# Four graph layers on one core: attention's bf16 adjacency masks are cast in layer 1 and kept in DRAM, and the first head's second half sums by comparisons

## The chip, the cores and the metric

The kernel runs on one core of one Trainium2 chip. The core has TensorE (PE, matrix products into PSUM), VectorE (DVE), ScalarE (ACT), GpSimd (POOL) and SyncE (SP), which work side by side and wait for each other by semaphores. SyncE, ScalarE and GpSimd also issue DMAs, each into a queue of its own; one set of 16 DMA engines serves all of them. The metric is the device time of one execution in microseconds, as the median of several runs. One execution was also taken with the hardware profiler; durations here come from it.

## The reference

x is 2708 x 512, `adj` is a symmetric 0/1 matrix of 2708 x 2708 with about 2.4% ones and a diagonal of ones. Four layers follow each other, each as `h = relu(layernorm(x)); x = x + layer(h, adj)`:

- layer 0: `relu((adj.T @ h) @ W * deg**-0.5)`;
- layer 1: the mean over the first 64 neighbours of each row, and two dense products with leaky ReLU;
- layer 2: graph attention with 8 heads of 64, the layer that this change is about;
- layer 3: the mean over all neighbours, and two dense products.

Layer 2, per head:

```python
Wh = h @ W                                   # 2708 x 64
e  = leaky_relu(f1[:, None] + f2[None, :], 0.2)   # f1 = Wh @ a1, f2 = Wh @ a2
p  = softmax(where(adj > 0, e, -9e15), axis=-1)
out = elu(p @ Wh)
```

## The kernel before

**Chunks.** Rows are cut into NC = 22 chunks of R = 128 (the last has 20). The adjacency is kept in SBUF as uint8, `vT[g][:, k, :]`: for each chunk m of neighbours, 2708 columns of nodes.

**Layer 1's aggregation.** `aggregate` walks seven spans of at most four chunks of columns; in each, for every m, `weight1(m, cs)` lets VectorE make a 128 x 512 weight `kt` (the first 64 neighbours), and TensorE multiplies by it into PSUM (`acc`). `after1` finishes the chunks of the span before, and `save2` stores them as x2 from ScalarE's queue. The tile `hT` (two buffers of the pool `common`) is used by the dense products before and after, not here.

**Attention.** The weight of neighbour m for node n is exp(leaky_relu(f1 + f2)) = exp(f2) * exp(0.2 f1) * max(exp(0.8 f1), exp(-0.8 f2)). `make(s)` lets VectorE compute `max(row, ec) * vT` in one instruction (tile `t2`, four buffers, line 1089); `scale(s)` lets ScalarE scale Wh by exp(f2) (`whs`, line 1073); `multiply(s)` multiplies the two on TensorE in four column groups of 32 (line 1348): `av` is the weighted sum, and `sums`, from one6, a column of ones, is the softmax's denominator.

A step s is one chunk m of one unit u. The units are head 0 in two parts (columns 0 to 1408, then 1300 more), heads 1 to 6 whole, and head 7 in two parts: 10 units of 22 steps. Weights are made three steps ahead. The last chunk's 20 rows of heads 1 to 6 are done together (`load_tails`, `exp_tails`, `make_tails`: `tails_row` is 120 x 2708).

**Sums by comparisons.** For chunks in `BY_SIDE` (17 of them, m % 5 != 2) of units 2 to 8 the f32 `sums` matmul is replaced: ScalarE makes a bf16 comparison tile b from the weight (`compare`, Sigmoid with a huge scale, line 1107), and `multiply_sides`, a step later, multiplies it by `parts`, exponentials split into three bf16 values, in bf16. What neighbours without comparison add is the same for every unit up to a factor per head, so `count_neighbors(i)` sums it once for all heads: the adjacency of chunk BY_SIDE[i] as bf16 (`mask(i, j)` for four quarters j of the columns, `fourths` = 0, 704, 1408, 2058, 2708) times `parts2`, into two PSUM banks `adj_sums`. Masks are cast from uint8 by ScalarE into one of five `x` tiles (line 1412); the last quarter of the later chunks is cast by VectorE into one of two `mask` tiles (line 1409). A count is 8 bf16 matmuls (line 1424).

**Order.** Steps are written out one after another; everything else hangs behind a step by `behind(step, fn, ...)`. `behind(1 + 39 * i // 16 + j // 2, mask, i, j)` and two steps behind the first `count_neighbors(i)` spread the 17 counts over the 44 steps of units 0 and 1. A scheduler then fixes the order of each engine's instructions from dependencies, this order as priority, and its own estimate of times; each engine works in that order. `issue_after` keeps an instruction behind another one.

Of the kernel before, what the change touches and what calls it, by code (L numbers as in the profile page):

```python
# [8 lines left out]
F32 = mybir.dt.float32  # L9
F32R = mybir.dt.float32r  # L10
BF16 = mybir.dt.bfloat16
# [9 lines left out]
P = 128  # L21

R = 128
# [21 lines left out]
def fast_layers(  # L45
# [36 lines left out]
    nc = tc.nc  # L82
    N, D = x_in.shape
    H, _, O = w2.shape
    NC = -(-N // R)
    NF = D // P
# [5 lines left out]
    def rows(c):  # L92
        return min(R, N - c * R)
# [17 lines left out]
    XBUFS = 5  # L111
    EARLY = NC // 2
# [8 lines left out]
    dram = ctx.enter_context(tc.tile_pool(name="dram", bufs=1, space=DRAM))  # L121

    common = ctx.enter_context(tc.tile_pool(name="common", bufs=2))
# [281 lines left out]
    vT = []  # L405
# [5 lines left out]
    where = {c: (g, k) for g, cs in enumerate(groups) for k, c in enumerate(cs)}  # L411

    def pattern(m, cs, n=R):

        g, k = where[m]
        v = vT[g][:n, k, cs[0] * R : (cs[-1] + 1) * R]
        return v.rearrange("p (c r) -> p c r", r=R)

    def by_chunk(t, cs):
        return t[:, : len(cs) * R].rearrange("p (c r) -> p c r", r=R)  # L420
# [56 lines left out]
    with ExitStack() as ring_ctx:  # L477
# [31 lines left out]
        with tc.tile_pool(name="l0", bufs=2) as wk, ExitStack() as ctx_l0:  # L509
            units = [(g, m) for g in range(len(groups)) for m in range(NC)]  # L510
# [364 lines left out]
        def fold(j):  # L875
# [9 lines left out]
                ALU.add,  # L885
            )

        def weight1(m, cs):
            kt = wk.tile([R, WG], F32R, name="kt", bufs=5)
            nc.vector.scalar_tensor_tensor(  # L890
                by_chunk(kt, cs),
                lastr[:, cs[0] * R : (cs[-1] + 1) * R].rearrange("p (c r) -> p c r", r=R),
                index[:R, m : m + 1],
                pattern(m, cs),
                op0=ALU.is_ge,
                op1=ALU.mult,
            )
            return kt
# [44 lines left out]

    BY_SIDE = [m for m in range(NC - 1) if m % 5 != 2]


    STEEP = 2.0**62
    ABOVE = 1.0 + 2.0**-21  # L950
    S = 32

    cut = EARLY * R // 8 * 8
    units = [(h, 0, N) for h in range(H)]
    units[-1:] = [(H - 1, 0, cut), (H - 1, cut, N)]
    units[:1] = [(0, 0, cut), (0, cut, N)]
# [3 lines left out]
    def in_tails(u, m):  # L960
# [2 lines left out]
    steps = [  # L963
        (u, m)
        for u in range(len(units))
        for m in ((NC - 1, *range(NC - 1)) if 1 < u < len(units) - 1 else range(NC))
    ]

    def by_side(u, m):
        return 1 < u < len(units) - 1 and m in BY_SIDE  # L970

    whd = dram.tile([N, D], F32, name="whd")
    avT = dram.tile([D, N], F32, name="avT")
# [15 lines left out]

    parts2 = at.tile([R, len(BY_SIDE), 2, H, 3], BF16, name="parts2")  # L990
    nc.gpsimd.memset(parts2, 0.0)
# [3 lines left out]
    row, weight, wh, whs, acc, sides, made, scaled = {}, {}, {}, {}, {}, {}, [], {}  # L995
# [52 lines left out]
    def load_wh(s):  # L1048
        u = steps[s][0]
        h = units[u][0]  # L1050
        t = at.tile([R, GROUP, O], F32, name="wh", bufs=3)
        ms = [m for v, m in steps[s : s + GROUP] if v == u and not in_tails(u, m)]
        full = [m for m in ms if m < NC - 1]
        k = len(full)
        for j, m in enumerate(sorted(ms)):
            wh[u, m] = t[:, j]
        if k:
            src = whd[full[0] * R : (full[0] + k) * R, h * O : (h + 1) * O]
            nc.sync.dma_start(t[:, :k], src.rearrange("(k p) o -> p k o", p=R))
        if k < len(ms):  # L1060
            src = whd[(NC - 1) * R :, h * O : (h + 1) * O]
            nc.sync.dma_start(t[:last_rows, k], src)

    def scale(s):

        u, m = steps[s]
        h, q = units[u][0], rows(m)
        if in_tails(u, m):
            whs[s] = tails_w[:LINES, middle.index(h)]
            return  # L1070
        t = at.tile([R, O + S], F32, name="whs", bufs=4)
        by = ef[:q, m, h : h + 1]
        ins = nc.scalar.activation(t[:q, :O], wh.pop((u, m))[:q], AF.Copy, scale=by)  # L1073
        if not by_side(u, m):
            ins = nc.scalar.activation(t[:q, O:], one6[:q], AF.Copy, scale=by)
        scaled[s] = ins.ins
        whs[s] = t[:q]

    def make(s):
        u, m = steps[s]  # L1080
        h, lo, hi = units[u]
        q = rows(m)
        g, k = where[m]
        if in_tails(u, m):
            weight[s] = tails_row[:LINES]
            made.append(made[-1])
            return
        t = at.tile([R, N], F32, name="t2", bufs=TILES)
        ins = nc.vector.scalar_tensor_tensor(  # L1089
            t[:q, : hi - lo],  # L1090
            row[h][:q, lo:hi],
            ec[:q, m, h : h + 1],
            vT[g][:q, k, lo:hi],
            op0=ALU.max,
            op1=ALU.mult,
        )
        weight[s] = t[:q]
        made.append(ins.ins)
# [91 lines left out]
    def split(first, end):  # L1190

        cs = slice(first, end)
        nc.scalar.mul(eb[:, cs], ec[:, cs], -STEEP * ABOVE)
        rest = common.tile([P, D], F32, name="rest", tag="t", bufs=3)
        rest = rest[:R, : (end - first) * H].rearrange("p (m h) -> p m h", h=H)
        for i in range(2):
            e = ef[:, cs]
            if i:
                nc.vector.tensor_tensor(rest, ec[:, cs], e, ALU.mult)
                e = rest  # L1200
            for k in range(3):
                part = parts_of[:, cs, :, 3 * i + k]
                nc.scalar.copy(part, e)
                if k < 2:
                    nc.vector.tensor_tensor(rest, e, part, ALU.subtract)
                    e = rest
        for i, heads in enumerate((slice(1, H), slice(1, H - 1))):
            kinds = sorted({m % 5 for m in BY_SIDE})
            for r in kinds:
                ms = [m for m in BY_SIDE if m % 5 == r and first <= m < end]  # L1210
                src = parts_of[:, ms[0] : ms[-1] + 1 : 5, heads, 3:6]
                at_i = [BY_SIDE.index(m) for m in ms]
                assert at_i == list(range(at_i[0], at_i[-1] + 1, len(kinds)))
                nc.scalar.copy(
                    parts2[:, at_i[0] : at_i[-1] + 1 : len(kinds), i, heads], src
                )
# [24 lines left out]
    def save_last2(c):  # L1241
# [7 lines left out]
    tails = tails_ctx.enter_context(  # L1249
        tc.tile_pool(name="tails", bufs=1, side="right", reuse_waits="tile")  # L1250
    )
# [140 lines left out]
                    t[j * step : j * step + height, : b - a],  # L1392
                )

    fourths = [0, cut // 2, cut, (cut + N) // 2, N]
    counted, masks = [], {}

    def pieces_of(j):
# [2 lines left out]
    def mask(i, j):  # L1401
        m = BY_SIDE[i]
        q = rows(m)
        g, k = where[m]
        own = slice(fourths[j], fourths[j + 1])
        n = own.stop - own.start
        if j == 3 and m >= EARLY:
            t = masks[i, j] = tails.tile([P, fourths[1]], BF16, name="mask", bufs=2)
            nc.vector.tensor_copy(t[:q, :n], vT[g][:q, k, own])
            return  # L1410
        t = masks[i, j] = common.tile([P, D], F32, name="x", bufs=XBUFS).bitcast(BF16)
        nc.scalar.copy(t[:q, :n], vT[g][:q, k, own])

    def count_neighbors(i):
        m = BY_SIDE[i]
# [37 lines left out]
    def behind(s, fn, *args):  # L1453
        plan.setdefault(s, []).append((fn, args))
# [5 lines left out]
    behind(10, load_row1, *units[1])  # L1460
    behind(9, split, EARLY, NC)
    behind(12, load_tails)
    behind(30, exp_tails)
    behind(36, make_tails)
    behind(30, load_l3_weights)
    behind(30, spread_nodes)
# [40 lines left out]
    for s in range(len(steps)):  # L1507
        if s == (len(units) - 3) * NC + 1:
            tails_ctx.close()
            first3 = ctx.enter_context(  # L1510
                tc.tile_pool(name="first3", bufs=1, side="right", reuse_waits="tile")
            )
            rings3 = [first3]
            b3 = first3.tile([P, D], F32, name="b3")
            nc.sync.dma_start(
                b3, bass.AP(tensor=bias3.tensor, offset=bias3.offset, ap=[[0, P], [1, D]])
            )
            e3_ctx = ctx.enter_context(ExitStack())
            e3 = e3_ctx.enter_context(
                tc.tile_pool(name="e3", bufs=2, side="right", reuse_waits="tile")  # L1520
            )
        if s + 6 < len(steps) and (s + 6) % NC % GROUP == 0:
            load_wh(s + 6)
        if s + 3 < len(steps):
            scale(s + 3)
            make(s + 3)
        if s + 1 < len(steps):
            compare(s + 1)
        multiply(s)
        multiply_sides(s - 1)  # L1530
        for fn, args in plan.pop(s, ()):
            if fn in (load_l3_weights, spread_nodes, split):
                with tc.issue_after(made[s]):
                    fn(*args)
            elif fn is mask:
                with tc.issue_after(scaled[s + 2]), tc.issue_after(made[s]):
                    fn(*args)
            else:
                fn(*args)
# [715 lines left out]
```

## Time and profile before

| | us |
|---|---|
| median of 3 runs | 1738.98 (1737.05 to 1739.90) |
| profiled execution, its own time | 1739.97 |
| profiled execution, span from first to last instruction | 1738.2 |
| first matmul of attention's unit 0, unit 1, unit 2 | 811.0, 860.0, 900.6 |
| TensorE busy | 1718.7 (99%) |
| VectorE busy | 1310.7 (75%) |
| ScalarE busy | 846.7 (49%) |
| GpSimd busy | 239.9 (14%) |
| DMA moved | 177.38 MB, mean 102 GB/s |

Times of instructions are counted from the span's start. Busy time is an average over stages, and the ends of the pipelined matmuls are modelled in the profile: TensorE at 99% does not say that TensorE is the limit everywhere. In rows of instructions in order of time, the bracket holds the engine's idle time before the instruction and what ended it. Records can overlap by some tens of nanoseconds where one instruction begins before the last has drained.

### The profile page before, as it was taken

What the parts mean: (1) busy time and instruction counts of PE and PEld (TensorE: products, weight loads), DVE (VectorE), ACT (ScalarE), POOL (GpSimd) and SP (SyncE); (2) the same over time, 40 slices, a digit from 0 to 9 for tenths busy, and PEclk for the clock granted to TensorE, in tenths of its full rate; (3) what the DMA queues carried; (4) which work ended last, traced back from release to release, by engine and by line L of the source; (5) the groups of instructions that cost most, each with busy time, mean ns of one, the idle gap of its engine ahead of it and who ended that gap; (6) DMA issues with size and microseconds to landing.
All of it is one profiled execution on the core that took longest, in us unless ns stands there. A gap on an engine that the chain in (4) does not pass through costs nothing.

```text
span 1738.2 us, 29482 instructions
## 1 busy us (share of the span) xinstructions
PE 1718.7 (99%) x11304; PEld 1074.6 (62%) x11304; DVE 1310.7 (75%) x1893; ACT 846.7 (49%) x1556; POOL 239.9 (14%) x246
## 2 busy tenths in 40 slices
PE   8999999999999999999999999999999999999998
PEld 5567777744458888644555676434434455588886
DVE  7759889865556756877899999999999777633334
ACT  5446767622210000266878888888885666400000
POOL 1003323311111111363000000000001222100000
PEclk9999999999999999999999999999999999999999
DMA  8436666444551111343420221122022444313221
GB/s 292 140 120 197 205 205 190 140 116 123 123 143 49 49 49 49 117 135 120 108 63 15 61 64 33 40 65 66 14 68 72 142 140 132 103 41 105 74 73 42
DMA packets 167228, 177.38 MB, mean 102 GB/s; under 512 B 84127, under 2 KB 106591, under 8 KB 166060
## 3 DMA queue, kind: packets, MB, share of 16 engines
q1 hardware_dynamic: 144428, 131.99, 27.2%
q10 hardware_dynamic: 18808, 33.37, 5.1%
q0 software_dynamic: 3840, 10.03, 1.5%
q8 instruction: 91, 1.49, 0.4%
q14 instruction: 61, 0.50, 0.1%
HBM read 111.64 MB, written 55.36 MB: 96 GB/s over the span
## 4 chain that ended last, share of the span: by engine, by line
PE 89%; DVE 6%; issue 2%; ACT 1%; SPq 1%; DMA 0%; DVEq 0%; ACTq 0%
PE acc L426 37%; PE av L1348 17%; PE nb_ps L188 8%; DVE t L1089 5%; PE h_ps L188 4%; PE wh_ps L188 4%; PE self_ps L188 4%; PE line_ps L188 4%; PE sums L1348 4%; PE hT_ps L247 2%; PE fused_ps L372 2%; ACT b L1107 1%; PE av_ps L1283 1%; DMA ws<-in_L_gnn_W_self 0%; PE sums_ps L633 0%
## 5 line engine op out<-in xcount | busy, mean ns | idle before, releaser
L1089 DVE SCALAR_TENSOR_TENSOR t<-rb,ec,vT 128x2708 f32<-128x2708 f32 (+2 forms) x214 | 513.2, 2457 | 12.5 <-PE sums L1348 9.8
L1348 PE MATMUL av<-t,whs 128*32 128x451 f32 (+5 forms) x4432 | 444.6, 514 | 3.4 <-DVE t L1089 2.1
L426 PE MATMUL acc<-halves,kt 128*128 128x512 f32 x1848 | 423.6, 390 | 1.0 <-DVE kt L890 1.0
L426 PEld LDWEIGHTS acc<-halves,kt 128*128 128x128 f32 x1848 | 346.0, 188 | 75.4 <-DVE kt L890 2.6
L1107 ACT ACTIVATE b<-t,eb 128x2708 bf16<-128x2708 f32 (+1 forms) x119 | 285.0, 2395 | 32.8 <-DVE t L1089 32.1
L1348 PEld LDWEIGHTS av<-t,whs 128*32 128x32 f32 (+1 forms) x4432 | 191.0, 110 | 165.3 <-issue 112.6
L426 PE MATMUL acc<-halves,ar 128*128 128x512 f32 x924 | 243.6, 414 | 0.0
L426 PEld LDWEIGHTS acc<-halves,ar 128*128 128x128 f32 x924 | 172.6, 188 | 58.2 <-issue 20.8
L224 ACT ACTIVATE ln_rs<-ln_mv,eps 128x1 f32<-128x1 f32 x88 | 25.7, 295 | 306.7 <-DMA x<-x 195.1
L890 DVE SCALAR_TENSOR_TENSOR kt<-lastr,index,vT 128x512 fp32r<-128x512 int16 (+3 forms) x154 | 110.6, 733 | 63.3 <-PE acc L426 62.9
L1572 DVE CAST kt<-vT 128x512 fp32r<-128x512 uint8 (+3 forms) x154 | 56.4, 368 | 130.7 <-PE acc L426 130.7
L1300 POOL TENSOR_SCALAR z<-y 128x512 f32<-128x512 f32 x22 | 44.1, 2006 | 642.2 <-DVE y L1293 642.2
L559 DVE TENSOR_TENSOR_SCAN cum<-ai,deg 128x512 int16<-128x512 int32 (+2 forms) x110 | 128.3, 1170 | 0.0
L602 ACT ACTIVATE cum<-cum,limit 128x512 int16<-128x512 int16 (+3 forms) x132 | 88.0, 667 | 52.0 <-DVE deg L567 49.8
L1348 PE MATMUL sums<-t,whs 128*32 128x325 f32 (+4 forms) x952 | 103.5, 448 | 0.0
L1073 ACT ACTIVATE whs<-wh,ef 128x64 f32<-128x64 f32 x214 | 72.7, 342 | 55.3 <-PE sums L1348 19.4
L220 DVE BATCH_NORM_STATS2 ln_st<-x 128x6 f32<-128x512 f32 x88 | 60.5, 689 | 48.9 <-DMA x<-x 34.9
L1348 PE MATMUL sums<-b,parts 128*32 128x338 bf16 (+2 forms) x884 | 76.8, 308 | 0.0
L188 PE MATMUL h_ps<-w0s,hT 128*128 128x512 f32 x168 | 75.8, 594 | 0.1
L188 PE MATMUL wh_ps<-w2s,hT 128*128 128x512 f32 x168 | 75.8, 594 | 0.0
L188 PE MATMUL self_ps<-wfs,hT 128*128 128x512 f32 x168 | 75.7, 593 | 0.0
L553 ACT ACTIVATE ar<-ai 128x512 fp32r<-128x512 int32 (+2 forms) x132 | 75.0, 568 | 1.4 <-DMA ai<-in_adj 0.9
(216 smaller groups left out, 1947.5 us busy)
## 6 DMA issues: line engine op xcount, KB each, us to landing
x<-x SPq DMA_DIRECT2D x105, 256.0 KB
ai<-in_adj SPq DMA_DIRECT2D x84, 256.0 KB
x<-x ACTq DMA_DIRECT2D x84, 256.0 KB
x<-in_x SPq DMA_DIRECT2D x42, 256.0 KB
rb<-rT SPq DMA_DIRECT2D x7, 1354.0 KB
wh<-whd SPq DMA_DIRECT2D x63, 96.0 KB
packed<-two POOLq DMA_DIRECT2D x44, 128.0 KB, 3.2
whd<-wh SPq DMA_DIRECT2D x21, 256.0 KB
```

The lines of the kernel that those rows point to most:

```text
L188: nc.tensor.matmul(po[:n], lhsT[:, f, :n], w[:, f, :], start=(f == 0), stop=(f == NF - 1))
L220: nc.vector.bn_stats(st[:n], xc[:n])
L426: nc.tensor.matmul(acc[:R], weight[:, k * R : (k + 1) * R], parts[:, i, :], start=(m == 0 and i == 0), stop=(m == NC - 1),)
L553: nc.scalar.activation(ar[:, :gw], ai[:, :gw], AF.Square, accum_out=squares[:R, m, g : g + 1])
L559: nc.vector.tensor_tensor_scan(cum[:n, :gw], ai[:n, :gw], ai[:n, :gw], 0.0 if g == 0 else deg[:n, m : m + 1], op0=ALU.add, op1=ALU.max,)
L602: nc.scalar.activation(cum[:n, :gw], cum[:n, :gw], AF.Sign, bias=limit[:n], scale=-1.0, accum_out=signs[:n, m, g : g + 1],)
L890: nc.vector.scalar_tensor_tensor(by_chunk(kt, cs), lastr[:, cs[0] * R : (cs[-1] + 1) * R].rearrange("p (c r) -> p c r", r=R), index[:R, m ...
L1073: ins = nc.scalar.activation(t[:q, :O], wh.pop((u, m))[:q], AF.Copy, scale=by)
L1089: ins = nc.vector.scalar_tensor_tensor(t[:q, : hi - lo], row[h][:q, lo:hi], ec[:q, m, h : h + 1], vT[g][:q, k, lo:hi], op0=ALU.max, op1=AL ...
L1107: nc.scalar.activation(b[:q, : hi - lo], weight[s][:, : hi - lo], AF.Sigmoid, bias=eb[:q, m, h : h + 1], scale=STEEP,)
L1348: nc.tensor.matmul(p[j * S : (j + 1) * S, : b - a], lhsT, rhs[:, part * size + a : part * size + b], start=(s % NC == 0), stop=(s % NC == ...
L1572: nc.vector.tensor_copy(by_chunk(kt, cs), pattern(m, cs))
```

## The change

1. All 68 masks (17 chunks x 4 quarters) are cast by ScalarE during layer 1's aggregation, one for each call of `weight1` from the 23rd on, into an `hT` tile, and stored from ScalarE's queue into a DRAM tensor `maskd`.
2. In attention `mask(i, j)` only loads: from `maskd` on GpSimd's queue, quarters 0 to 2 into `x` tiles, the last into a `mask` tile. ScalarE's and VectorE's casts are gone there, and so is the `issue_after` that held masks behind the scaling and the weight of a step.
3. Unit 1 (head 0's second part) also sums by comparisons for the 17 chunks; its last, 20-row chunk comes first, as in the later units, and `parts2` is filled for head 0 as well.
4. `exp_tails` hangs behind step 20 and not 30.

```diff
+        maskd = dram.tile([len(BY_SIDE), R, N], BF16, name="maskd")
+        asked = []
+        def widen(n):
+            i, j = divmod(n, 4)
+            g, k = where[BY_SIDE[i]]
+            own = slice(fourths[j], fourths[j + 1])
+            t = common.tile([P, NF, R], F32, name="hT").rearrange("p f r -> p (f r)")
+            t = t.bitcast(BF16)[:R, : own.stop - own.start]
+            nc.scalar.copy(t, vT[g][:R, k, own])
+            nc.scalar.dma_start(maskd[i, :, own], t)
+
         def weight1(m, cs):
+            if NC <= len(asked) < NC + 4 * len(BY_SIDE):
+                widen(len(asked) - NC)
+            asked.append(m)
             kt = wk.tile([R, WG], F32R, name="kt", bufs=5)
...
-        for m in ((NC - 1, *range(NC - 1)) if 1 < u < len(units) - 1 else range(NC))
+        for m in ((NC - 1, *range(NC - 1)) if 0 < u < len(units) - 1 else range(NC))
...
-        return 1 < u < len(units) - 1 and m in BY_SIDE
+        return 0 < u < len(units) - 1 and m in BY_SIDE
...
-        for i, heads in enumerate((slice(1, H), slice(1, H - 1))):
+        for i, heads in enumerate((slice(1, H), slice(0, H - 1))):
...
     def mask(i, j):
-        if j == 3 and m >= EARLY:
-            t = masks[i, j] = tails.tile([P, fourths[1]], BF16, name="mask", bufs=2)
-            nc.vector.tensor_copy(t[:q, :n], vT[g][:q, k, own])
-            return
-        t = masks[i, j] = common.tile([P, D], F32, name="x", bufs=XBUFS).bitcast(BF16)
-        nc.scalar.copy(t[:q, :n], vT[g][:q, k, own])
+        if j == 3:
+            t = tails.tile([P, N - fourths[3]], BF16, name="mask", bufs=2)
+        else:
+            t = common.tile([P, D], F32, name="x", bufs=XBUFS).bitcast(BF16)
+        masks[i, j] = t
+        nc.gpsimd.dma_start(t[:q, :n], maskd[i, :q, own])
...
-    behind(30, exp_tails)
+    behind(20, exp_tails)
...
-            elif fn is mask:
-                with tc.issue_after(scaled[s + 2]), tc.issue_after(made[s]):
-                    fn(*args)
```

`BY_SIDE`, `cut` and `fourths` are defined earlier in the file than before, with the same values.

More of the change, by code (lines that the diff above doesn't have):

```diff
@@ L886, in fold @@
             )
+        BY_SIDE = [m for m in range(NC - 1) if m % 5 != 2]
+        cut = EARLY * R // 8 * 8
+        fourths = [0, cut // 2, cut, (cut + N) // 2, N]
+        maskd = dram.tile([len(BY_SIDE), R, N], BF16, name="maskd")
[8 more added lines that the diff above has]
+            nc.scalar.dma_start(maskd[i, :, own], t)
         def weight1(m, cs):
+            if NC <= len(asked) < NC + 4 * len(BY_SIDE):
+                widen(len(asked) - NC)
+            asked.append(m)
             kt = wk.tile([R, WG], F32R, name="kt", bufs=5)
@@ L936, in fast_layers @@
         aggregate(weight1, h1, before1, after1, lead=4, ahead=ahead)
-    BY_SIDE = [m for m in range(NC - 1) if m % 5 != 2]
     STEEP = 2.0**62
@@ L951, in fast_layers @@
     S = 32
-    cut = EARLY * R // 8 * 8
     units = [(h, 0, N) for h in range(H)]
@@ L1393, in evict @@
                 )
-    fourths = [0, cut // 2, cut, (cut + N) // 2, N]
     counted, masks = [], {}
@@ L1403, in mask @@
         q = rows(m)
-        g, k = where[m]
         own = slice(fourths[j], fourths[j + 1])
         n = own.stop - own.start
-        if j == 3 and m >= EARLY:
-            t = masks[i, j] = tails.tile([P, fourths[1]], BF16, name="mask", bufs=2)
-            nc.vector.tensor_copy(t[:q, :n], vT[g][:q, k, own])
-            return
-        t = masks[i, j] = common.tile([P, D], F32, name="x", bufs=XBUFS).bitcast(BF16)
-        nc.scalar.copy(t[:q, :n], vT[g][:q, k, own])
+        if j == 3:
[4 more added lines that the diff above has]
+        nc.gpsimd.dma_start(t[:q, :n], maskd[i, :q, own])
     def count_neighbors(i):
```

## The prediction

> **What bounds the kernel now.** I read the page first, then busy time by stretch, then VectorE's and TensorE's instructions in order of time between 810 and 910 us, then GpSimd's DMAs. A "step" s is one chunk m of one unit u: steps 0 to 21 are head 0's first 1408 columns (unit 0), 22 to 43 its other 1300 (unit 1), then come whole heads. From the page (engine, busy, share; group, busy, mean ns, idle before it):
>
> ```profile
> PE 1718.7 (99%) x11304; PEld 1074.6 (62%) x11304; DVE 1310.7 (75%) x1893; ACT 846.7 (49%) x1556; POOL 239.9 (14%) x246
> L1089 DVE SCALAR_TENSOR_TENSOR t<-rb,ec,vT 128x2708 f32<-128x2708 f32 (+2 forms) x214 | 513.2, 2457 | 12.5 <-PE sums L1348 9.8
> ```
>
> TensorE looks full everywhere, so the stage decides. Busy time by stretch (length, PE, PEld, DVE, ACT, POOL, clock, DMA share, GB/s) and VectorE in order of time:
>
> ```profile
> 810.00:859.00 49.00, 46.54 (x620) 25.59 (x615) 36.66 (x30) 39.65 (x106) 0.00 (x0) 1.00 0.38 100
> 860.00:898.00 38.00, 37.95 (x560) 24.10 (x564) 37.01 (x28) 28.92 (x71) 0.00 (x0) 0.96 0.29 83
> 863.74 1.57 DVE L1089 SCALAR_TENSOR_TENSOR t<-rb,ec,vT 128x1300 f32<-128x1300 f32 x1
> 865.22 0.50 DVE L1409 CAST mask<-vT 128x650 bf16<-128x650 uint8 x1
> 865.63 3.14 DVE L1089 SCALAR_TENSOR_TENSOR t<-rb,ec,vT 128x1300 f32<-128x1300 f32 x2
> 895.42 11.89 DVE L1089 SCALAR_TENSOR_TENSOR t<-rb,ec,vT 128x2708 f32<-128x2708 f32 x4 [0.36 <-PE sums L1348]
> 908.10 411.45 DVE L1089 SCALAR_TENSOR_TENSOR t<-rb,ec,vT 128x2708 f32<-128x2708 f32 x155 [0.79 <-PE av L1348]
> ```
>
> From 908.1 to 1319.5 VectorE's weights run without one idle gap: VectorE is the bound of heads 1 to 7, and whatever moves its start at 908 moves the end by as much. In unit 0 TensorE paces (VectorE 36.7 of 49). In unit 1 both are nearly full (37.95 and 37.01 of 38). TensorE's own holes, and what they waited for:
>
> ```profile
> 836.46 0.44 PE L1424 MATMUL adj_sums<-x,parts 128*24 128x325 bf16 x5 [1.68 <-ACT x L1412]
> 841.84 0.30 PE L1424 MATMUL adj_sums<-x,parts 128*24 128x325 bf16 x1 [0.62 <-ACT x L1412]
> 859.16 0.47 PE L1424 MATMUL adj_sums<-x,parts 128*24 128x352 bf16 x4
> 860.04 2.13 PE L1348 MATMUL av<-t,whs 128*32 128x325 f32 x16 [0.42 <-ACT whs L1073]
> ```
>
> 2.3 us of unit 0 wait for ScalarE's mask casts, and step 22 starts at 860.04, 0.8 us after step 21's end at 859.2.
>
> **Part by part.** The base is the profiled execution: span 1738.2, its own time 1739.97, which is 0.99 over the median 1738.98.
>
> (1) Casts in layer 1: 68 ScalarE casts at 0.72 to 0.76 us (the rows of the same cast at line 1412) and 68 stores from its queue at 0.33. ScalarE does nothing there (0.00 of 20 us in each stretch from 520 to 700), TensorE runs beside it. The cover is the two-tile ring: a cast waits for the store two before. With the landing of GpSimd's stores below, two casts take 0.72 + 0.33 + 3.2 = 4.3 us, 68 take 146 us, and from 546 to 720 there are 174. Cost nothing. Without this cover ScalarE's stores of x2, queued behind, come late (rival 3).
>
> (2) First head's second half by comparisons: 17 steps lose four f32 matmuls (0.55 us for the four, in the chain of waits) and get four bf16 ones: 0.31 if only one runs at a time beside others, 0.15 if as in the counts, where eight take 0.29 (817.98 to 818.27). TensorE saves 17 x 0.24 to 17 x 0.40 = 4.1 to 6.8 us in unit 1. ScalarE gets 17 comparisons, 1.45 us for 1408 columns, so about 1.35: 23 us, in place of some 26 casts (19 us). Its 28.9 of 38 busy stay under 35.
>
> (3) VectorE loses 8 casts; one costs 0.43 (868.68 to 869.11), 7 of them after 863.74 cost 3.0. What is late next there: a 1300-column weight is 1.57 long and 1.49 apart when nothing holds it (118 weights of 2708 columns are 3.03 long and 2.95 apart). From step 26's weight (863.74) to step 45's (895.42) are 31.7 us; 18 weights need 26.8, TensorE's steps 18 x 1.09 + 4 x 0.55 + 14 x 0.31 + 7 counts x 0.4 = 28.9 at most. I take 27.7: this stretch gets shorter by 4.0 (3.0 to 4.9).
>
> (4) Unit 0: the masks no longer come from ScalarE, so the 2.3 us go and step 21 ends at T = 856.9. The first seven mask loads stand among GpSimd's products for f12 before 808: 7 x 0.54 = 3.8 us, and GpSimd has 11.8 of 30 us free from 780 to 810 (busy 4.83, 7.52 and 5.87 of 10). Nothing; without that room the start of unit 0 moves by up to 3.8.
>
> (5) What it costs. The order in which the changed program's instructions stand shows that TensorE has, after step 21 and ahead of step 22, 34 adj_sums matmuls in a row: the counts 8 to 11 and a quarter of 12. Before, half a count stood there. Their 34 matmuls are about 4 us, but their masks must be loaded first, into five x tiles and two mask tiles, which are freed by these very matmuls. After count 7 (T - 1.8, a step of 1.78 before T) 14 more loads have to be issued in order from GpSimd's queue, and the first tile of count 12 is the third user of its buffer: load, matmul, load, matmul, load. Step 22 and everything behind it on TensorE waits for that. The nearest row is GpSimd's DMA of 128 KB in layer 0 (issue ns min/median/max; to landing from the start of the issue), against 162 to 176 KB here:
>
> ```profile
> L619 POOL DMA_DIRECT2D packed<-two x66: 539/539/782, 16.6 to 341.3; - x66
> DMA to landing us min/median/max: 1.9/3.2/10.1
> 863.19 0.35 SPq L1002 DMA_DIRECT2D rb<-rT  x1
> ```
>
> Low end: 13 issues of 0.54 and a landing of 1.9: T - 1.8 + 7.0 + 1.9 = T + 7.1. Three landings in a row at 3.2 and 0.3 between: T + 8.1. High end: the load of head 1's row (1354 KB, SyncE's queue, 4 us after step 21) shares the 16 DMA engines; stretches of 20 us with one show 0.38 to 0.43 DMA share, without 0.04 to 0.07, so it is 6.6 us at most: T + 14.7. I take T + 10, a third of that overlap: step 22 starts at 866.9. Step 26's weight needs its buffer: 1.7 us at full clock, 3.7 as it was (0.83 granted from 860 to 870); with 2.0 it starts at 868.9, so 5.2 later than 863.74 (865.7 to 875.3: 2.0 to 11.6 later). VectorE has cover for only part: it is four weights ahead, and the tails' 3.0 us lie in that gap in both kernels.
>
> The Trainium skill speaks against the queue: "SBUF — State Buffer", Who interferes with whom, says that a VectorE copy or cast in a two-port mode shuts GpSimd out and with it the writing of its DMA descriptors; another place there puts a DMA of 620 ns at 3100. The rows of issue above (782 ns at most, beside a busy VectorE) do not show it, and the change takes VectorE's casts out of this stretch; by the rule 11 loads would add some 27 us. "DMA: Bandwidth & Descriptors", Anatomy of one DMA, gives 2.0 us plus bytes over 436 GB/s, so 2.4 for a mask (an estimate from that page) where the row says 3.2; with it the sum would be 2 us lower.
>
> (6) Into head 1 VectorE idles 0.79 at 908, where ScalarE loads the comparison's table and evicts the counts:
>
> ```profile
> 897.49 1.28 ACT L1107 ACT_TABLE_LOAD   x1
> 901.25 3.62 ACT L1438 COPY out<-adj_sums 24x352 f32<-24x352 f32 x8
> ```
>
> The table now comes at step 23, under the pile; the evictions stay. Gain 0 to 0.8, taken 0.4. The earlier exp_tails is one ScalarE group of about 1 us, and its last load is issued by 836; nothing. Step 22 is now the 20-row chunk: same length, nothing.
>
> Sum: + 5.2 - 4.0 - 0.4 = + 0.8, so 1740.8 on the profiled base, 1739.8 as a median. The parts of TensorE's saving beyond 4.0 are hidden behind VectorE.
>
> **Rivals.** *Slower: the pile decides.* From step 22's start at 869.6 on (T + 12.7), the sum is over + 3.5. For it: the row load falls into the pile, the masks keep the engines busy by themselves, landings went up to 10.1. At the high end + 11.6 - 3.0 = + 8.6: 1747.6; in the middle 1745. *Faster: the loads keep up.* If masks land before they are needed, the tails' weights and not the pile hold step 26: 856.9 + 1.6 + 3.0 = 861.5, 2.2 earlier, so - 2.2 - 4.0 - 0.4 = - 6.6: 1732.4. Against it: 14 issues alone last 7.6 us. *Layer 1 is hit.* With landings over 4.1 us the 68 casts outlast their 174 us and delay x2; 6.4 would put them 80 us over, and the time some tens of us up. Against: a DMA share of 0.01 to 0.34 there.
>
> **How the numbers follow.** About 0.2% (3.5 us) is what a measurement of this kernel can tell; the three times spread over 2.85. My forecast, no change that can be told, gets 0.47; the slower rival 0.28 and layer 1 0.05, so slower 0.33; faster 0.20. The range is the ends of the unknown costs, + 2.0 - 4.9 - 0.8 = - 3.7 and + 8.6, cut a little above and opened below toward the fast rival: 1734.5 to 1746.5.
>
> **What would show it.** In the changed profile: no TensorE wait for ScalarE's casts from 818 to 857; a run of adj_sums matmuls with waits for DMA between about 857 and 867, step 22's first matmul at 864 to 871; step 26's weight 2 to 8 us later than 863.74; then 18 weights in 27 to 29 us and no VectorE idle until 1320; a span from 908 on of the same length. I am wrong if masks hold TensorE in unit 0 as well, if VectorE is not gapless after the pile, or if unit 0 starts later than 811.

## The result, and the profile after

The changed kernel takes 1755.44 us (median of 5 runs, 1755.41 to 1759.33), the kernel before 1738.80 (5 runs beside them): a ratio of 1.0102, 95% interval 1.0091 to 1.0114. It is slower by 16.6 us. The profiled execution took 1755.95, its span is 1754.2.

From the page of the changed kernel (engine, busy, share; then groups: busy, mean ns, idle before and what ended it):

```profile
PE 1720.9 (98%) x11236; PEld 1028.1 (59%) x11236; DVE 1306.0 (74%) x1885; ACT 876.9 (50%) x1564; POOL 276.3 (16%) x314
L1104 DVE SCALAR_TENSOR_TENSOR t<-rb,ec,vT 128x2708 f32<-128x2708 f32 (+2 forms) x214 | 511.7, 2462 | 31.2 <-PE sums L1363 28.5
L901 ACT CAST hT<-vT 128x704 bf16<-128x704 uint8 (+1 forms) x68 | 50.8, 756 | 62.9 <-DMA maskd<-hT 47.0
```

The sums per engine hardly moved. What moved is VectorE's idle time before its weights: 31.2 us where it was 12.5. Busy time by stretch (length, PE, PEld, DVE, ACT, POOL, clock, DMA share, GB/s), cut at the end of step 21 and the start of step 22:

```profile
811.50:866.00 54.50, 47.94 (x617) 22.68 (x614) 36.01 (x28) 22.94 (x77) 17.04 (x32) 0.94 0.66 185
866.00:882.20 16.20, 7.82 (x34) 1.27 (x29) 4.44 (x2) 2.80 (x7) 8.43 (x16) 0.58 0.92 289
882.20:918.00 35.80, 35.63 (x527) 20.87 (x526) 32.75 (x20) 28.38 (x46) 7.59 (x14) 0.95 0.48 140
```

Unit 0 takes 54 us, where it took 48; then come 16 us in which TensorE runs nothing but counting matmuls, half the time none; unit 1 is short. In unit 0 the DMA share (the busy share of the 16 DMA engines) is 0.66 (0.38 before), in the pile 0.92. TensorE in order of time, the bracket with its idle time and what ended it:

```profile
849.51 0.31 PE L1437 MATMUL adj_sums<-x,parts 128*24 128x352 bf16 x1 [0.98 <-DMA x<-maskd]
851.95 0.31 PE L1437 MATMUL adj_sums<-x,parts 128*24 128x352 bf16 x1 [2.13 <-DMA x<-maskd]
855.34 0.43 PE L1437 MATMUL adj_sums<-x,parts 128*24 128x325 bf16 x1 [3.08 <-DMA x<-maskd]
...
855.61 2.80 PE L1363 MATMUL av<-t,whs 128*32 128x352 f32 x16
...
865.08 0.77 PE L1363 MATMUL sums<-t,whs 20*32 20x352 f32 x8
...
872.82 0.43 PE L1437 MATMUL adj_sums<-x,parts 128*24 128x325 bf16 x1 [3.31 <-DMA x<-maskd]
...
876.39 2.05 PE L1437 MATMUL adj_sums<-x,parts 128*24 128x352 bf16 x6 [2.85 <-DMA x<-maskd]
...
882.26 1.30 PE L1363 MATMUL av<-t,whs 20*32 20x325 f32 x16
```

Every one of these waits is for a mask's load: 6.2 us in unit 0, 8.1 in the pile (three short ones of 0.45, 0.86 and 0.65 are not shown). Step 21 ends at 865.8, step 22 starts at 882.26. VectorE, four weights ahead, stops twice for long, then twice for 0.5 us, and from 888.26 on runs to the end of its weights without a gap:

```profile
859.62 1.56 DVE L1104 SCALAR_TENSOR_TENSOR t<-rb,ec,vT 20x1300 f32<-20x1300 f32 x1 [9.33 <-PE sums L1363]
884.17 1.57 DVE L1104 SCALAR_TENSOR_TENSOR t<-rb,ec,vT 128x1300 f32<-128x1300 f32 x1 [13.74 <-PE sums L1363]
888.26 447.18 DVE L1104 SCALAR_TENSOR_TENSOR t<-rb,ec,vT 128x1300 f32<-128x1300 f32 x175 [0.44 <-PE sums L1363]
```

884.17 is step 26's weight (863.74 before, so 20.4 later). The gapless run ends at 888.26 + 447.18 = 1335.4; before it ended at 908.10 + 411.45 = 1319.6. These 15.9 us are the whole difference of the spans (16.0).

Why do masks come late? GpSimd's DMAs issued from 838.5 to 850, then those from 899 to 915 (time from issue to landing):

```profile
L1425 POOL DMA_DIRECT2D x<-maskd x6: 548/548/548, 839.7 to 846.4; - x6
...
DMA to landing us min/median/max: 4.5/10.6/12.3
```

```profile
DMA to landing us min/median/max: 2.6/2.9/3.9
```

The issue itself always takes 0.55 us; the landing goes from 3 to 10 us. At 839.8 to 843.0 SyncE issued unit 1's row (650 KB) and the six rows of the tails (211 KB each), 1.9 MB in all; at 869.8, in the pile, head 1's row of 1354 KB. The kernel before issued the same 1.9 MB at the same time, and the DMA engines were 0.72 busy there without any mask load:

```profile
839.68 0.37 SPq L1002 DMA_DIRECT2D rb<-rT  x1
840.10 2.32 SPq L1019 DMA_DIRECT2D tails_row<-rT  x6
840.00:850.00 10.00, 9.38 (x133) 6.16 (x126) 7.58 (x7) 9.36 (x29) 0.00 (x0) 1.00 0.72 177
```

With the mask loads beside them the share is 0.94 from 840 to 848.

### The profile page after: what moved, and what is told of

Same layout as the page of the kernel before. It is cut to its first block, busy times and chain, and to the rows that moved or that the text cites. A ratio compares the mean times of both kernels' runs of the same rounds, so it can differ in the third digit from the quotient of the medians.

```text
span 1754.2 us, 29608 instructions
## 1 busy us (share of the span) xinstructions
PE 1720.9 (98%) x11236; PEld 1028.1 (59%) x11236; DVE 1306.0 (74%) x1885; ACT 876.9 (50%) x1564; POOL 276.3 (16%) x314
## 4 chain that ended last, share of the span: by engine, by line
PE 82%; DVE 9%; issue 5%; DMA 2%; ACT 1%; POOL 1%; SPq 0%; DVEq 0%; ACTq 0%; POOLq 0%
PE acc L426 37%; PE av L1363 12%; DVE t L1104 8%; PE nb_ps L188 8%; PE h_ps L188 4%; PE wh_ps L188 4%; PE self_ps L188 4%; PE line_ps L188 4%; PE sums L1363 3%; PE hT_ps L247 2%; PE fused_ps L372 2%; DMA x<-maskd 1%; ACT b L1122 1%; PE av_ps L1298 1%; POOL x L1425 0%
## 5 line engine op out<-in xcount | busy, mean ns | idle before, releaser
L1104 DVE SCALAR_TENSOR_TENSOR t<-rb,ec,vT 128x2708 f32<-128x2708 f32 (+2 forms) x214 | 511.7, 2462 | 31.2 <-PE sums L1363 28.5
L1363 PE MATMUL av<-t,whs 128*32 128x451 f32 (+4 forms) x4432 | 426.4, 516 | 3.6 <-DVE t L1104 2.6
L1122 ACT ACTIVATE b<-t,eb 128x2708 bf16<-128x2708 f32 (+2 forms) x136 | 308.3, 2267 | 45.6 <-DVE t L1104 45.2
L1363 PEld LDWEIGHTS av<-t,whs 128*32 128x32 f32 (+1 forms) x4432 | 153.5, 110 | 195.3 <-issue 154.2
L901 ACT CAST hT<-vT 128x704 bf16<-128x704 uint8 (+1 forms) x68 | 50.8, 756 | 62.9 <-DMA maskd<-hT 47.0
L188 PE MATMUL nb_ps<-wfn,hT 128*128 128x512 f32 x168 | 75.6, 593 | 0.0
```

The source lines that it names most:

```text
L188: nc.tensor.matmul(po[:n], lhsT[:, f, :n], w[:, f, :], start=(f == 0), stop=(f == NF - 1))
L1104: ins = nc.vector.scalar_tensor_tensor(t[:q, : hi - lo], row[h][:q, lo:hi], ec[:q, m, h : h + 1], vT[g][:q, k, lo:hi], op0=ALU.max, op1=AL ...
L1122: nc.scalar.activation(b[:q, : hi - lo], weight[s][:, : hi - lo], AF.Sigmoid, bias=eb[:q, m, h : h + 1], scale=STEEP,)
L1363: nc.tensor.matmul(p[j * S : (j + 1) * S, : b - a], lhsT, rhs[:, part * size + a : part * size + b], start=(s % NC == 0), stop=(s % NC == ...
```

## The experiments

Theory 1: the masks' loads hold TensorE, because they share the DMA engines with the broadcast rows, and because five `x` tiles let only the next count's masks be under way; the pile ahead of step 22 makes it worse. Rivals: the order alone; the new comparisons; the casts in layer 1; the turnaround of the tiles without any rows. All runs stand beside runs of the kernel before, whose median lay between 1737.9 and 1739.0.

**e1, the pile undone.** `multiply` keeps its last instruction in `done[s]`.

```diff
+            elif fn is count_neighbors:
+                with tc.issue_after(done[s].ins):
+                    fn(*args)
```

> The changed kernel with one thing undone: each count of neighbours keeps its place behind the matmuls of the step it was planned at, so no 34 counting matmuls stand together ahead of step 22; loads, queue and buffers as changed. Theory 1 (masks that land late hold TensorE, and the pile multiplies it): the 6.2 us of waits in unit 0 (849.5 to 855.3) stay, the 8 us of waits between 866 and 882 shrink to 2 or less, the time is 1744 to 1748. Theory 2 (the order alone costs the 16 us): 1736 to 1740. Theory 3 (each load costs its wait wherever its count stands): 1753 to 1757.

Measured: 1748.69, ratio 1.0057 (1.0040 to 1.0073): 6.8 under the changed kernel. Unit 0's waits are 6.0 us (2.83 and 3.14), as theory 1 expected; after 866 waits of 4.4 us are left, where it expected 2 or less, and the time lies 0.7 above its range. The order is worth 6.8 of the 16.6, with loads.

**e2, the loads left out**, with e1's tie.

```diff
+        if i + j:
+            masks[i, j] = masks[0, 0]
+            return
+        t = tails.tile([P, fourths[1]], BF16, name="mask", bufs=1)
```

> As e1, but 67 of the 68 mask loads are left out: every count reads the first mask tile (the counted sums are then those of one chunk's quarter). Theory 1: without loads no TensorE wait for masks is left, the time is 1731 to 1736, and what it lies below the kernel before is what the removed casts and the comparisons in unit 1 are worth (5 to 7 us by the working of the prediction, 6.6). Rival (the comparisons in unit 1 or the casts in layer 1 cost time themselves): 1740 or above in spite of it.

Measured: 1733.28, ratio 0.9971 (0.9960 to 0.9983). This is in theory 1's range. The loads cost 15.4 us in e1's order, and everything else in the change gains 4.6. So the comparisons and layer 1's casts together are no cost. One new wait is there, of TensorE at step 22:

```profile
857.23 1.33 PE L1364 MATMUL av<-t,whs 20*32 20x325 f32 x16 [2.08 <-ACT whs L1089]
```

ScalarE has the comparison's table, the first two comparisons and unit 0's evictions ahead of the scaling there.

**e10, loads left out and the pile kept**: e2 without the tie. The order then puts 72 counting matmuls ahead of step 22.

> The changed kernel with 67 of 68 mask loads left out as in e2, and no tie: the order then puts 72 counting matmuls (nine counts) ahead of step 22, twice the changed kernel's pile. Theory 1: a pile without loads costs TensorE only its matmuls, 9 x 0.55 = 5 us at once, of which VectorE's four weights ahead cover most, and unit 1 gets them back: 1733 to 1737. Rival (a pile of this length costs by itself, loads or not): 1740 or more.

Measured: 1730.44, ratio 0.9952 (0.9937 to 0.9968), faster than e2 and below theory 1's range of 1733 to 1737. TensorE in order of time:

```profile
855.74 2.86 PE L1437 MATMUL adj_sums<-mask,parts 128*24 128x352 bf16 x72
858.53 1.30 PE L1363 MATMUL av<-t,whs 20*32 20x325 f32 x16
```

72 matmuls take 2.86 us, and ScalarE's table, comparisons and evictions lie under them, so the 2.08 of e2 is not there. Here a pile is no loss; a pile of matmuls that wait for loads is. With its loads the same change is 25.0 us slower (1755.44 less 1730.44, with nine counts in the pile and not four and a quarter).

**e3, the comparisons alone**: the kernel before with unit 1's three edits of the diff, masks cast as before.

> The kernel before with the comparisons in unit 1 alone: masks cast by ScalarE and VectorE as before, nothing in layer 1, the tails' exponentials where they were. Theory 1: comparisons are no loss; ScalarE gets some 23 us more work in a stretch of 38 in which it is busy 29 with casts, so counts come later and VectorE's stretch hardly shortens: 1736 to 1740. Rival (comparisons in unit 1 cost): 1745 or above, with TensorE waiting for sums of ScalarE in unit 1.

Measured: 1745.89, ratio 1.0040 (1.0026 to 1.0054): the rival's side. (Unit 0 starts 1.5 us later there, at 812.3 where it was 810.9; that part comes ahead of any comparison.) Stretch from 880 to 900:

```profile
880.00:900.00 20.00, 19.18 (x277) 11.80 (x269) 16.69 (x15) 20.00 (x31) 0.00 (x0) 1.00 0.05 12
```

ScalarE (fourth) is busy 20.00 of 20, and VectorE waits for its comparisons (`ACT b`). The comparisons need the casts out of unit 1, which the change does; it is no cost of the change.

**e4, the tails' loads hung behind step 26.**

```diff
-    behind(12, load_tails)
-    behind(20, exp_tails)
+    behind(26, load_tails)
+    behind(30, exp_tails)
```

> The changed kernel with the loads for the tails (six rows of 211 KB and their small ones) at step 26 instead of 12, their exponentials at 30 instead of 20. With that the counts stand one to a few steps again (no pile), and the rows do not fall beside the mask loads of 840 to 855. Theory 1 with the rows as the reason of the late landings in unit 0: both losses go, 1733 to 1739, with under 1.5 us of TensorE waits for masks before step 22. Rival (GpSimd's queue or the turnaround of the buffers is slow by itself): waits of 4 us or more in unit 0 stay, 1743 to 1748.

Measured: 1748.66, ratio 1.0060 (1.0043 to 1.0077). The time lies nearest to the rival's range, but the edit did not do what it was meant for: the pile is gone, while SyncE still issued two rows at 840.9 (unit 1's and head 1's) and four tails' rows from 843.8 to 851.9. So it says no more than e1. **e5** was to hold the rows back better.

```diff
+    behind(23, load_tails_rows)
...
-            if fn in (load_l3_weights, spread_nodes, split):
+            if fn in (load_l3_weights, spread_nodes, split, load_tails_rows):
                 with tc.issue_after(made[s]):
```

> e1 with the six row loads of the tails (211 KB each) tied behind the weight of step 23, so that they can't be issued at 840, where they and the 650 KB row of unit 1 stand beside the masks of counts 7 and 8. Theory 1a (a mask lands late because it shares the DMA engines with these loads): the masks issued at 844 land in 3 to 6 us and not 10 to 11, the 6.0 us of waits in unit 0 fall to 3 or less, 1743 to 1746. Rival 1b (the turnaround of five x tiles and GpSimd's queue are too slow for TensorE's pace by themselves): the waits stay, 1748 to 1750.

Measured: 1750.86, ratio 1.0065 (1.0048 to 1.0081), just above the rival's range, and inconclusive for the same reason: `issue_after` orders the scheduler's list, and SyncE, with nothing to wait for, issued five of the rows from 841.8 to 851.2. The next runs leave rows out.

**e9, e12, e14: rows left out one after another**, in e1's order; a constant set by GpSimd stands in each row's place.

```diff
-            nc.sync.dma_start(
-                tails_row[own],
-                bass.AP(tensor=src.tensor, offset=src.offset, ap=[[0, last_rows], [1, N]]),
-            )
+    nc.gpsimd.memset(tails_row, 1.0)
```

> e1 with the six row loads of the tails (6 x 211 KB) left out, the tile set to a constant by GpSimd before unit 0 instead; so the tails' weights are made from that constant. In e5 the tie did not hold these loads: they were issued at 842 to 851 all the same. Theory 1a (a mask lands late because it shares the DMA engines with these rows): the masks issued at 844 land in 3 to 7 us and not 10 to 11, the 6.0 us of waits in unit 0 fall to 3 or less, 1743 to 1746. Rival 1b (buffers and queue by themselves are too slow): landing under 5 us, waits stay above 4, 1748 or more. Rival 1c (the 650 KB row of unit 1 alone does it): landing stays 8 or more, 1747 to 1749.

```diff
-    behind(10, load_row1, *units[1])
+            if h == 0:
+                nc.gpsimd.memset(row[h][:, hi:], 1.0)
```

> e9 with the 650 KB row of unit 1 left out too (a constant in its place, set by GpSimd), so that no broadcast load is in flight while unit 0 counts. In e9 the masks issued at 844 still landed in 7.9 to 9.6 us. Theory 1a (sharing the DMA engines with rows is all of it): they land in 2.5 to 5 us, waits in unit 0 under 0.7 us in all, 1737 to 1740; what is left are the waits of unit 1. Rival 1b (turnaround of the x tiles at TensorE's pace): waits of 2 us or more stay in unit 0 though landings are short, 1741 or more.

```diff
+            if h == 1:
+                nc.gpsimd.memset(row[h], 1.0)
+                return
```

> e12 with head 1's row (1354 KB) left out as well: in e9 and e12 SyncE's queue, emptier, issued it at 840 instead of 869, so it stood beside the masks of unit 0 in place of the rows left out. Now no broadcast row is loaded from 840 to head 2. Theory 1a: the masks issued at 844 land in 2.5 to 4 us, the waits of unit 0 after 840 are under 0.5 us, and the time lies between the 1733.3 of e2 (no loads) and the 1738.2 of e12; what it lies above e2 is the price of the masks' own turnaround. Rival 1b: over 1.5 us of waits in unit 0 though landings are under 4 us, and 1738 or more.

Measured: e9 1741.89, ratio 1.0018 (1.0009 to 1.0028); e12 1738.25, ratio 1.0003 (0.9994 to 1.0012); e14 1737.58, ratio 0.9998 (0.9989 to 1.0008). Landings of the masks issued from 838.5 to 850, in e1, e9, e12 and e14:

```profile
DMA to landing us min/median/max: 3.6/10.9/12.0
```

```profile
DMA to landing us min/median/max: 2.6/7.9/9.6
```

```profile
DMA to landing us min/median/max: 2.6/3.0/7.3
```

```profile
DMA to landing us min/median/max: 2.5/2.9/3.5
```

What was in flight beside them: in e1 1.9 MB of rows; in e9 2.0 MB (unit 1's row, and head 1's, which SyncE's emptier queue issued at 841 and no longer in unit 1); in e12 1.35 MB (head 1's); in e14 no row. TensorE's waits for masks from 840 to 857 are 6.0, 2.7, 1.7 and 0 us. So in unit 0 the rows in flight are all of it, and theory 1a stands. That the two share the time of the DMA engines, and not something else on the way from DRAM, is argued from the engines' busy share: from 840 to 848 it is 0.99 in e1 and 0.50 in e14. Of e9's own expectation neither side held, since another row moved in, and for the same reason e12's 1.7 us lie between its two sides. e14 still waits for 4.9 us of masks in unit 1, with landings of at most 4.1: there GpSimd issues a load only after TensorE has released it (at 863.63 for the longest wait, which ends at 866.38), which is the turnaround of the tiles. Behind the 4.3 us that e14 lies above e2 stand these waits and the 2.0 us by which GpSimd's constant delays the first masks at 821 (a side effect of the edit); how much of each shows in the time is not known.

As a ladder: 1755.4 as changed; less 6.8 for the pile (e1); less 6.8 for the tails' rows and for head 1's row out of unit 1 (e9); less 3.6 and 0.7 for the other rows (e12, e14); less 4.3 for the loads themselves: 1733.3 (e2). The intervals of these ratios reach 1.6 to 3 us to either side, so the 0.7 can't be told from nothing. Not tried is issuing the loads from another engine; in unit 0 they had GpSimd's queue to themselves, and still landed late.

**e6, e15, e11: the counts moved into the heads**, where VectorE is the bound. Only the step of the first mask changes, from `1 + 39 * i // 16`:

```diff
+        first = 46 + 4 * i          # e6
+        first = 46 + 2 * i          # e15
+        first = 43 + 5 * i // 4     # e11
```

> The changed kernel with the counts planned in heads 1 to 4: the first at step 46 and one every four steps, not one every 2.4 steps from step 1. There VectorE is the bound, one count has 11.8 us, and no broadcast row but the next head's is loaded. Theory 1: no TensorE wait for a mask of more than 0.5 us delays a weight, units 0 and 1 lose their counts as well (8 of 0.55 us in unit 0): 1727 to 1731. Rival (the two PSUM banks that the counts hold make each change of head wait for evictions, 0.5 to 1.5 us for each of four): 1733 to 1738.

> e6 with a count every two steps instead of four (first at step 48, last at 80): 5.9 us for a count whose issue and landing take 5.4, and one change of head (step 66) with the counts' two banks held instead of two. Theory: it saves one of e6's idles of VectorE at such changes (3.66 and 1.46 us): 1733 to 1735. Rival (as in e11 the loads then hold TensorE past VectorE's four weights): 1738 or more.

> The changed kernel with the counts within head 1 (first at step 45, one every 1.25 steps, the last at step 65), so that their two PSUM banks are free again before the change to head 2; in e6 VectorE idled 3.66 and 1.46 us at two such changes. Theory: VectorE idles under 1.5 us from step 30 to the end of the weights; a count has 3.7 us, four issues last 2.2 and a landing 3 more, so TensorE waits for some masks, but behind VectorE's four weights: 1729 to 1733, below both kernels. Rival (the loads are too dense for one head): over 4 us of VectorE idle in head 1, 1735 to 1740.

Measured: e6 1736.49, ratio 0.9989 (0.9979 to 0.9998); e15 1736.74, ratio 0.9992 (0.9983 to 1.0001); e11 1748.61, ratio 1.0059 (1.0045 to 1.0073). e6's time is in the rival's range, and VectorE stops at changes of head,

```profile
1024.66 62.05 DVE L1104 SCALAR_TENSOR_TENSOR t<-rb,ec,vT 128x2708 f32<-128x2708 f32 x21 [3.66 <-PE av L1363]
```

and for 1.46 us at the next one. That the banks do it is shown only in part. Ahead of the first stop TensorE waits 1.80 us for a mask's load (until 1022.58), against theory 1's 0.5, and 0.26 for an eviction; ahead of the second it waits 0.55 for an eviction. e15 holds the banks over one change only and idles 4.95 us there, but after a wait of 3.30 for a mask at 961.7, so it gains nothing on e6, and its time lies between theory and rival. e11, slower than even its rival said, shows that a stage with VectorE as bound hides loads only up to a rate: a count every 1.25 steps brings 16 us of VectorE idle between 932 and 977 (4.19, 0.75, 7.04 and 4.34), of which two rows:

```profile
936.96 5.99 DVE L1104 SCALAR_TENSOR_TENSOR t<-rb,ec,vT 128x2708 f32<-128x2708 f32 x2 [4.19 <-PE sums L1363]
965.89 6.07 DVE L1104 SCALAR_TENSOR_TENSOR t<-rb,ec,vT 128x2708 f32<-128x2708 f32 x2 [7.04 <-PE av L1363]
```

**e7, e8: e6's places with masks cast by ScalarE**, no DRAM copy; e7 with the comparisons in unit 1, e8 without.

```diff
-        if j == 3 and m >= EARLY:
+        if j == 3:
             t = masks[i, j] = tails.tile([P, fourths[1]], BF16, name="mask", bufs=2)
-            nc.vector.tensor_copy(t[:q, :n], vT[g][:q, k, own])
+            nc.scalar.copy(t[:q, :n], vT[g][:q, k, own])
```

> The kernel before with comparisons in unit 1 and the counts of e6's places, but masks cast by ScalarE (all four quarters) and no DRAM copy. Theory: ScalarE has room there (a comparison of 2.27 and a scaling of 0.34 in a step of 2.95, five steps of 22 without comparison), so it is as fast as e6: 1727 to 1732. Rival (ScalarE's casts delay comparisons and so weights): 1735 to 1745. The difference to e6 is what the loads are worth in a place where they cost no wait.

> e7 without the comparisons in unit 1: the kernel before with its counts in e6's places, masks cast by ScalarE. Theory: unit 0 wins its 2.3 us of waits and some 4 us of counts, unit 1 its casts on VectorE; what e7 lies below it is the comparisons' worth (TensorE 4 to 7 us in unit 1, most of it hidden behind VectorE): 1729 to 1734. Rival (the counts in units 0 and 1 were hidden): 1737 to 1740.

Measured: e7 1739.01, ratio 0.9999 (0.9990 to 1.0009); e8 1738.04, ratio 0.9996 (0.9986 to 1.0005). Both expectations of a gain failed: what units 0 and 1 save is given back at the changes of head (VectorE idles 4.30 and 2.55 us in e7, 3.32 and 2.51 in e8). Here no loads are in play, and TensorE waits for evictions at the first of these changes, 2.7 us in e7 and 1.7 in e8; the changed kernel, with no count there, has no such wait. So holding the banks does cost. In e7 the casts may add to it: ScalarE is busy 20.00 of 20 us from 1000 to 1020 (17.49 in e6), since a comparison of 2708 columns takes 2.55 us and not 2.27 as expected. Between the two no worth of the comparisons shows. Loads in place of the casts take 2.5 us less in these places (e6 against e7), a difference at the edge of the intervals.

**e13, split**: nine counts in unit 0 with ScalarE's casts as before, eight in head 1 with loads.

```diff
+    CAST = 9
+        if i < CAST:
+            nc.scalar.copy(t[:q, :n], vT[g][:q, k, own])
+        else:
+            nc.gpsimd.dma_start(t[:q, :n], maskd[i, :q, own])
+        first = 1 + 39 * i // 16 if i < CAST else 45 + 5 * (i - CAST) // 2
```

> The changed kernel with its first nine counts in unit 0 at their old steps and their masks cast by ScalarE as before, and its other eight counts in head 1 (first at step 47, one every 2.5 steps) with masks loaded. Unit 1 has no counts, and no mask is loaded while a row of units 0 or 1 is. Theory: unit 0 as in the kernel before (its 2.3 us of waits included), unit 1 at VectorE's pace, a count of head 1 has 7.4 us for loads that take 5.4, no head changes with the counts' banks held: 1732 to 1736. Rival (the loads in head 1 hold TensorE past VectorE's four weights as in e11): 1738 or more.

Measured: 1736.58, ratio 0.9993 (0.9984 to 1.0002), between theory and rival: no wait for a mask's load is left, VectorE runs gapless from 866.3, and TensorE's wait for ScalarE at step 22 is 2.31 us. Of the versions that compute everything, only e6's interval lies wholly below the kernel before, by 0.1%.

## Why the prediction was wrong

It said 1739.8 (1734.5 to 1746.5), no change that can be told the likeliest; measured 1755.4. It had loads that hold TensorE ahead of step 22, too small, and none that hold it in unit 0. By its steps:

1. *Casts in layer 1 cost nothing*: right. They run from 505 to 621 us. TensorE is busy 40.00 of 40 us in each stretch from 520 to 640 in both kernels. ScalarE's casts wait 47 us for their own stores; TensorE waits for none of them. Unit 0 starts at 811.5, where it was 810.9; with the same casts it starts at 810.75 in e1 and 810.86 in e2, without them at 812.3 in e3. So the sign "unit 0 starts later than 811" came, but inside what runs differ by.
2. *TensorE's saving by comparisons is hidden*: nothing speaks against it (e7 against e8).
3. *From step 26's weight to step 45's 27.7 us*: right. 884.17 to 912.23 is 28.1; it was 31.7.
4. *Unit 0 loses the 2.3 us of waits, step 21 ends at 856.9*: **this step failed.** Without loads it holds (in e10 step 21 ends at 855.7). With them TensorE waits 6.2 us for masks in unit 0, then runs at a lower clock, and step 21 ends at 865.8: 8.9 too little. The prediction named "masks hold TensorE in unit 0 as well" as a sign of being wrong, but had no term for it: the landing was taken as 3.2 us from a row of layer 0, for the pile alone, and in unit 0 the loads were put at nothing; I did not ask which other loads are in flight when each mask is. The 1.9 MB of rows at 840 stood in the trace of before, on SyncE's queue (shown above). And where TensorE paces, a wait has no cover.
5. *The pile, T + 10*: the term was there, named as the likely place of a loss, and too small. Measured: 865.8 to 882.26, T + 16.5, beyond even its high end of T + 14.7. (That end took 6.6 us at most for head 1's row; the shares it names, 0.43 less 0.04 of 20 us, allow 7.8, which would still be short.) The matmuls are less than I took (72 in 2.86 us, e10), the waits more: 8.1 us, with landings up to 7.0 beside head 1's row, which I had priced at a third of its 6.6 us. In e10 a pile of 72 is done 2.8 us after step 21, so at most that much of the 16.5 is the pile's own work.
6. *Into head 1 without the idle 0.79*: right. The table's load comes under the pile as said; without the pile it costs 2.08 us at step 22 (e1, e2).

The sum: step 26's weight was put at 868.9 and came at 884.17, 15.3 later (8.9 of unit 0 and 6.5 of the pile, less 0.1 from step 22 to it). With +0.8 for the whole, 0.4 more for step 3 and 0.5 less at the entry into head 1 that makes 16.0, the difference of the spans. The faster rival's condition, that masks are there when needed, gives 1733.3 and 1730.4 where it is made true (e2, e10); the rival said 1732.4. So 4.6 to 8 us of gain are in the change (1737.93 less 1733.28, 1738.71 less 1730.44), and the loads take them and 16.6 more.

Of the rules weighed there: the page "SBUF — State Buffer", Who interferes with whom, has VectorE's casts stretch GpSimd's DMAs; no run shows it here, the changed kernel's issues take 548 to 594 ns throughout, and the changed kernel has no such casts in this stretch, so nothing here tests it. The estimate from "DMA: Bandwidth & Descriptors", 2.4 us, agrees with a mask alone (2.5 at least, 2.9 median in e14). The rule that mattered is another section of that page, Issuing engines are not separate DMA queues: DMAs from GpSimd and SyncE run on the same 16 engines and interleave. This case agrees, with 3.5 us at most for a mask alone (e14, from 838.5 to 850) and 12.3 beside 1.9 MB.

## What to carry to other kernels

Before a cast is turned into a load, list every DMA that is in flight when each load is, on all queues, and take the landing from a row with that company; 3 us alone was 10 here. An engine that works in order and is the bound of its stage pays a late load in full, and matmuls that pile up ahead of the next step cost what their loads cost, not what they are. A queue whose loads are moved or left out issues its next loads earlier, and those may land in the same place.

## What the runs showed of the hardware

TensorE's granted clock fell where it waited, which I had not counted: 0.50 from 872 to 880 (PE busy 4.20 of 8 us, the clock is the last number but two),

```profile
872.00:880.00 8.00, 4.20 (x16) 0.70 (x16) 0.00 (x0) 0.00 (x0) 3.30 (x7) 0.50 0.96 324
```

and after the waits of unit 0, with 0.50 granted from 856 to 859, sixteen matmuls of a step took 2.80 us (at 855.61, shown above), where they take 1.38 at full clock. The two steps from 855.61 to 861.59 take 5.98 us, where two take 3.55 in e10. So step 21 ends 10.0 us later than in e10: 6.2 of waits, 2.4 of lower clock, and smaller parts such as matmuls that run singly between the waits. The Trainium skill's "TensorE: Matmul & The Clock Gate", Part 1, says that the clock is halved after an idle window of about 3.4 us and comes back after as long a busy one; the 0.50 agrees, but no wait in unit 0 is that long: here 2.13 and 3.08 us with a single matmul of 0.31 between them were enough. From 862 to 866 the full clock is granted again.
